# A circulant recurrence rebuilt: from a doubling tree over all sequences to one scan along time per sequence, pipelined over sequences

## The chip, the cores and the metric

The kernel runs on one NeuronCore of a Trainium2 chip. The metric is the device time of one launch in microseconds (us), taken as the median of several executions. Beside it there is one profiled execution, whose trace gives every instruction with its engine, its line in the kernel, its start and its duration. PE is TensorE (matmuls), DVE is VectorE, ACT is ScalarE, POOL is GpSimd and SP is SyncE, which issues DMAs here. All data is fp32.

## What is computed

Eight sequences of 512 tokens with 128 features (`u`) go through a chain of residual blocks: a linear recurrence with a circulant transition matrix, a LoRA feed-forward network, a four-layer encoder with linear attention, LoRA again, causal attention, a mixture of experts, a gated linear recurrence, and experts again. Only the first block changes:

```
z    = layernorm(x)
h_t  = W h_{t-1} + B z_t          # W orthogonal and circulant, 128 x 128
x   += C h_t + D z_t
```

`W` is the Cayley transform of a skew circulant matrix. Its eigenvalues are `(1 - w^2 - 2iw) / (1 + w^2)`, of modulus 1, with `w` from a Fourier sine sum over 63 parameters. In the Hartley basis (cosine plus sine) each frequency is a plain rotation by an angle, so powers of `W` are cosines and sines of multiples of that angle.

## The kernel before

`net_kernel` issues the input loads, runs `rotate_block` for the recurrence, then enters `encoder_block`, which holds LoRA and the encoder as pipelines over sequences. A pipeline (`pieces`) takes a generator for each sequence and a list of ages; in each round it advances several sequences by one step each, in the listed order, and after every so many steps it may advance a second stream, its `side`. LoRA runs with `LORA = (-2, 0, 1, -1, 0, -1, 1, -1, -2)`, and from its round 6 on the encoder's stream is its side. Inside `encoder_block` everything stands under `in_program_order`: each of PE, DVE, ACT and POOL executes its instructions in the order in which the code writes them.

`rotate_block` stands outside that order. It works on all eight sequences at once, in five parts:

- The norm of each sequence (`zin`, lines 169, 170, 156, 157, 187), the transpose to features by time (`flip`, L196, copied by L148) and the product with `B` (L234, copied by L150 into `h`).
- Cosine and sine of the rotation angle, starting from a matmul with the sine table (L242) and followed by small DVE operations (L243 to L249), then eight angle doublings (L253 to L258).
- Nine weight matrices, one for each power of two of `W` (L268 to L271 on DVE, L275 and L276 on PE, L277).
- A doubling tree along time: nine levels up and eight levels down, each a matmul (L287) and an addition (L288) on strided columns of `h`. The wide levels work on every second column, the narrow ones on one or a few columns per sequence.
- The output: products with `C` and with a diagonal of `D` (L301, L302), added to `x` (`add_x`, L219).

LoRA's steps on a sequence are the norm (`norm_start`, `norm_end`, where every second piece runs on ACT, L183), a bias added on POOL (L216), the transpose and four selections (L196, L333), `left` and `e` (L339, L341, L350), two small outer products (L356) added to the weights (`w1e` L359, `w2e` L360), then the network (L366, L367, L374) and `add_x`.

The queues at the start: SP issues `u` in eight parts (L2160), then the encoder's weights `e`, the blank fills of the expert slots (L966) and `l`. ACT's queue issues `ident`, `col`, `f` (LoRA's weights) and `a` (the recurrence's weights). POOL's queue issues `lnf`, `row` and `erow`. Rotation weights have a pool of their own (`w_a`). `ps` gives PSUM tiles; the usual banks are four of tag a, two of b and two of c.

Of the kernel before, what the change touches and what calls it, by code (L numbers as in the profile page):

```python
# [19 lines left out]
P = 128  # L20
B = 8
# [68 lines left out]
class Net:  # L90
# [30 lines left out]

    def load(self, name, pool=None, queue=None, parts=1, rows=None):

        dram = self.drams[name]
        n = dram.shape[1]
        if rows:
            dram = dram.to_broadcast([rows, n])
        t = (pool or self.const).tile([dram.shape[0], n], dram.dtype, name=f"w_{name}")
        step = -(-n // parts)
        for at in range(0, n, step):  # L130
            to = min(at + step, n)
            (queue or self.nc.sync).dma_start(t[:, at:to], dram[:, at:to])
        fields = {}
        for key, (at, shape) in self.offsets[name].items():
            v = t[:, at : at + math.prod(shape)]
            if len(shape) == 2:
                v = v.rearrange("p (a b) -> p a b", b=shape[1])
            elif len(shape) == 3:
                v = v.rearrange("p (a b c) -> p a b c", b=shape[1], c=shape[2])
            fields[key] = v  # L140
        self.packs[name] = fields
        return fields
# [16 lines left out]
    def norm(self, src, dst, n=NT, split=False):  # L159

        self.norm_end(src, dst, self.norm_start(src, n), split)

# [11 lines left out]
    def norm_end(self, src, dst, found, split=False):  # L174
# [6 lines left out]
        for t in range(n):  # L181
            if split and t % 2:
                nc.scalar.activation(  # L183
# [37 lines left out]

def rotate_block(k):

    nc, tc = k.nc, k.tc
    w = k.packs["a"]
    lv = 9
    with tc.tile_pool(name="rot", bufs=1, reuse_waits="tile") as pool, tc.tile_pool(name="rot_t", bufs=2, reuse_waits="tile") as tmp:
        h = pool.tile([P, B, S], F32, name="h")
        zt = pool.tile([P, B, S], F32, name="zt_all")
        for b in range(B):  # L230
            z = k.zin(b)
            k.flip(z, zt[:, b, :])
            pu = k.ps([P, S])
            nc.tensor.matmul(pu, w["bw"], zt[:, b, :], start=True, stop=True)  # L234
            k.evac(h[:, b, :], pu)


        cs = pool.tile([P, lv], F32, name="cs")
        sn = pool.tile([P, lv], F32, name="sn")
        t = pool.tile([P, 6], F32, name="eig")  # L240
        pp = k.ps([P, 1], "c")
        nc.tensor.matmul(pp, w["sin"], w["a"], start=True, stop=True)  # L242
        nc.vector.tensor_copy(t[:, 0:1], pp)  # L243
        nc.vector.tensor_tensor(t[:, 1:2], t[:, 0:1], t[:, 0:1], ALU.mult)
        nc.vector.tensor_scalar(t[:, 2:3], t[:, 1:2], 4.0, 1.0, ALU.mult, ALU.add)
        nc.vector.reciprocal(t[:, 3:4], t[:, 2:3])
        nc.vector.tensor_scalar(t[:, 4:5], t[:, 1:2], -4.0, 1.0, ALU.mult, ALU.add)
        nc.vector.tensor_tensor(cs[:, 0:1], t[:, 4:5], t[:, 3:4], ALU.mult)
        nc.vector.scalar_tensor_tensor(sn[:, 0:1], t[:, 0:1], 4.0, t[:, 3:4], ALU.mult, ALU.mult)  # L249
        sq = pool.tile([P, 2 * lv], F32, name="eig_sq")  # L250
        for i in range(1, lv):
            c0, s0 = cs[:, i - 1 : i], sn[:, i - 1 : i]
            nc.vector.tensor_tensor(sq[:, 2 * i : 2 * i + 1], s0, s0, ALU.mult)  # L253
            nc.vector.tensor_tensor(sq[:, 2 * i + 1 : 2 * i + 2], c0, c0, ALU.mult)
            nc.vector.tensor_tensor(
                cs[:, i : i + 1], sq[:, 2 * i + 1 : 2 * i + 2], sq[:, 2 * i : 2 * i + 1], ALU.subtract
            )
            nc.vector.scalar_tensor_tensor(sn[:, i : i + 1], c0, 2.0, s0, ALU.mult, ALU.mult)  # L258


        ra = pool.tile([P, lv, P], F32, name="ra")
        rb = pool.tile([P, lv, P], F32, name="rb")
        wt = pool.tile([P, lv, P], F32, name="wt")
        for i in range(lv):
            c0, s0 = cs[:, i : i + 1], sn[:, i : i + 1]
            u = tmp.tile([P, P], F32, name="u")
            v = tmp.tile([P, P], F32, name="v")
            nc.vector.tensor_scalar(u, w["sin"], s0, None, ALU.mult)  # L268
            nc.vector.scalar_tensor_tensor(ra[:, i, :], w["cos"], c0, u, ALU.mult, ALU.subtract)
            nc.vector.tensor_scalar(v, w["cos"], s0, None, ALU.mult)  # L270
            nc.vector.scalar_tensor_tensor(rb[:, i, :], w["sin"], c0, v, ALU.mult, ALU.add)  # L271
        for at in range(0, lv, 4):
            n = min(4, lv - at)
            pw = k.ps([P, n, P], "c")
            nc.tensor.matmul(pw, w["cos"], ra[:, at : at + n, :], start=True, stop=False)  # L275
            nc.tensor.matmul(pw, w["sin"], rb[:, at : at + n, :], start=False, stop=True)  # L276
            nc.vector.tensor_scalar(wt[:, at : at + n, :], pw, 1.0 / P, None, ALU.mult)  # L277

        def level(i, first, count):

            d = 1 << i
            seqs = min(max(1, S // count), B // 2)
            for b in range(0, B, seqs):
                to = h[:, b : b + seqs, first : first + (count - 1) * 2 * d + 1 : 2 * d]
                of = h[:, b : b + seqs, first - d : first - d + (count - 1) * 2 * d + 1 : 2 * d]
                ph = k.ps([P, seqs, count])
                nc.tensor.matmul(ph, wt[:, i, :], of, start=True, stop=True)  # L287
                nc.vector.tensor_tensor(to, to, ph, ALU.add)  # L288

        for i in range(lv):  # L290
            level(i, (2 << i) - 1, S >> (i + 1))
        for i in range(lv - 2, -1, -1):
            level(i, (3 << i) - 1, (S >> (i + 1)) - 1)

        dg = pool.tile([P, P], F32, name="dg")
        nc.vector.tensor_scalar(dg, k.ident, k.col["D"], None, ALU.mult)
        for b in range(B):
            py = k.ps([P, NT, D])
            for t in range(NT):
                at = slice(t * P, (t + 1) * P)  # L300
                nc.tensor.matmul(py[:, t, :], h[:, b, at], w["cw"], start=True, stop=False)  # L301
                nc.tensor.matmul(py[:, t, :], zt[:, b, at], dg, start=False, stop=True)  # L302
            k.add_x(b, py)

# [112 lines left out]
def encoder_block(k, before, behind):  # L417
# [7 lines left out]
    with tc.tile_pool(name="enc1", bufs=1, reuse_waits="tile") as one, tc.tile_pool(name="enc", bufs=2, reuse_waits="tile") as pool:  # L425
# [158 lines left out]
        with in_program_order(tc):  # L584
# [9 lines left out]
            stream = counted()  # L594
            before(pool, stream)
            for _ in stream:
# [1559 lines left out]
def net_kernel(ctx: ExitStack, tc: tile.TileContext, drams, offsets, out):  # L2156
    nc = tc.nc
    k = Net(ctx, tc, drams, offsets)
    for b in range(B):
        nc.sync.dma_start(k.xb(b), drams["u"][b].rearrange("(t p) d -> p t d", p=P))  # L2160
    k.ident = k.load("ident", queue=nc.scalar)["ident"]
    k.col = k.load("col", queue=nc.scalar)
    k.mhalf = k.const.tile([P, 8], F32, name="mhalf")
    nc.gpsimd.memset(k.mhalf, -0.5)
    k.lnf = k.const.tile([P, 2, D], F32, name="lnf")
    nc.gpsimd.dma_start(k.lnf.rearrange("p a d -> p (a d)"), drams["lnf"].to_broadcast([P, 2 * D]))
    k.all1 = k.const.tile([P, P], F32, name="all1")
# [8 lines left out]
    saved = tc.dram_tile([P, B * NT * D], F32, name="saved")  # L2176

    w_e, w_a = ExitStack(), ExitStack()
    p_e = w_e.enter_context(tc.tile_pool(name="w_e", bufs=1))
    p_a = w_a.enter_context(tc.tile_pool(name="w_a", bufs=1))  # L2180
    rooms, own, w_f = ExitStack(), ExitStack(), ExitStack()
    room = rooms.enter_context(tc.tile_pool(name="moe1", bufs=1, side="right", reuse_waits="tile"))
    p_l = own.enter_context(tc.tile_pool(name="w_l", bufs=1, side="right", reuse_waits="tile"))
    ready = p_l.tile([P, S], F32, name="zt0")
    k.load("f", w_f.enter_context(tc.tile_pool(name="w_f", bufs=1, side="right")), nc.scalar)
    work = ExitStack()
    work.enter_context(k.working())
    k.load("a", p_a, nc.scalar)
    k.row = k.load("row", queue=nc.gpsimd, rows=P)
    k.load("erow", p_e, nc.gpsimd, rows=P)  # L2190
    k.load("e", p_e, parts=2)
    usual = dict(a=4, b=2, c=2)
    banks = dict(attention=dict(a=1, b=1, c=1, s=2, o=1), after=dict(a=3, b=2, c=3), experts=dict(a=4, b=2, y=2), gated=usual)
    flat = k.x.rearrange("p t d -> p (t d)")

    with k.banks(**usual):
        rotate_block(k)
    w_a.close()
    slots = [blank_slots(k, one) for one in GROUPS]
# [11 lines left out]

    def before(pool, side):
        pipeline(lora_steps(k, lambda: pool), B, LORA, side=side, every=1, first=B - 2)

# [91 lines left out]
def _constants():  # L2306
# [4 lines left out]
    ang = 2.0 * np.pi * ((i[:, None] * i[None, :]) % P) / P  # L2311
    c["cos"], c["sin"] = np.cos(ang).astype(f), np.sin(ang).astype(f)
    pick = np.zeros((P, 4, 4), f)
# [40 lines left out]
def _layout(inp):  # L2354
# [10 lines left out]
    a = Pack(P)  # L2365
    a.add("cos", c["cos"])
    a.add("sin", c["sin"])
    a.add("bw", ae("B_w").T)
    a.add("cw", ae("C_w").T)
# [114 lines left out]
```

## Time and profile before

| | |
|---|---|
| median of 3 runs | 1958.11 us (1957.21 to 1969.49) |
| profiled execution | 1991.02 us, its span 1989.3 us, mean granted TensorE clock 0.921 |
| busy, share of the span | PE 86%, DVE 65%, ACT 48%, POOL 37% |
| last `add_x` of the recurrence (L219) | starts at 92.47 us |
| LoRA's first L366 | starts at 98.03 us |
| blank fills, issue on SP (L966) | 14.54 to 69.22 us |

The profile's views used here are the windows (busy time of each engine in stretches of the span, with the granted clock and the DMA rate), the timeline (instructions in order of time; the brackets give the idle time before an instruction and what ended it) and the groups (instructions of one line and shape: count, total busy us and mean ns after the bar, then the idle time before them). Durations and positions are those of the profiled execution, which took 1.7% longer than the median.

### The profile page before, as it was taken

What the parts mean: (1) busy time and instruction counts of PE and PEld (TensorE: products, weight loads), DVE (VectorE), ACT (ScalarE), POOL (GpSimd) and SP (SyncE); (2) the same over time, 40 slices, a digit from 0 to 9 for tenths busy, and PEclk for the clock granted to TensorE, in tenths of its full rate; (3) what the DMA queues carried; (4) which work ended last, traced back from release to release, by engine and by line L of the source; (5) the groups of instructions that cost most, each with busy time, mean ns of one, the idle gap of its engine ahead of it and who ended that gap; (6) DMA issues with size and microseconds to landing.
All of it is one profiled execution on the core that took longest, in us unless ns stands there. A gap on an engine that the chain in (4) does not pass through costs nothing.

```text
span 1989.3 us, 30025 instructions
## 1 busy us (share of the span) xinstructions
PE 1710.9 (86%) x10171; PEld 1164.1 (59%) x10171; DVE 1289.3 (65%) x4211; ACT 957.5 (48%) x1737; POOL 730.3 (37%) x866
## 2 busy tenths in 40 slices
PE   4998899999998798999989877888898878789895
PEld 2655678878776555444444445665555535567664
DVE  7666888888886765566667445337555784565463
ACT  1034556666654432566555543435544444454453
POOL 2022333333333522444444753643202216145543
PEclk9898999999998898899999889989998777899998
DMA  9800000000000011000000021122001001111341
GB/s 259 161 1 1 1 1 1 1 1 1 1 1 1 17 77 43 1 1 1 1 1 1 24 72 33 57 83 62 20 7 36 17 3 36 42 42 58 91 118 57
DMA packets 79391, 71.26 MB, mean 36 GB/s; under 512 B 6560, under 2 KB 73120, under 8 KB 78336
## 3 DMA queue, kind: packets, MB, share of 16 engines
q1 hardware_dynamic: 69120, 47.89, 9.7%
q0 software_dynamic: 9536, 20.47, 3.1%
q8 instruction: 86, 1.41, 0.3%
q10 hardware_dynamic: 576, 0.90, 0.1%
q14 instruction: 73, 0.60, 0.1%
HBM read 34.98 MB, written 34.25 MB: 35 GB/s over the span
## 4 chain that ended last, share of the span: by engine, by line
PE 29%; DVE 14%; ACT 7%; issue 5%; POOL 1%; another core or an unknown queue 1%; DMA 1%; DVEq 0%; POOLq 0%; ACTq 0%; SPq 0%
PE ps_a L1320 4%; PE ps_a L1321 3%; PE ps_s L715 3%; PE ps_y L1293 3%; PE ps_b L1284 2%; PE ps_o L744 2%; DVE sh L1709 2%; DVE x L1370 2%; PE ps_c L935 1%; ACT pr L725 1%; PE ps_a L1727 1%; DVE half L1333 1%; DVE hid L1334 1%; PE ps_a L1293 1%; PE ps_a L1878 1%
## 5 line engine op out<-in xcount | busy, mean ns | idle before, releaser
L157 POOL TENSOR_TENSOR ln_rs<-rs_v,mhalf 128x4 f32<-128x4 f32 x144 | 150.3, 1045 | 393.7 <-DVE rs_v L156 381.9
L1217 POOL DMA_INDIRECT given<-yr,to x163 | 158.8, 974 | 287.8 <-PE ps_a L1320 76.7
L1333 DVE SCALAR_TENSOR_TENSOR half<-half,ps_a 128x352 f32<-128x352 f32 x163 | 84.5, 518 | 202.7 <-ACT half L1326 163.4
L725 ACT ACTIVATE pr<-ps_s 128x1024 f32<-128x1024 f32 x160 | 154.7, 1019 | 125.7 <-PE ps_s L715 118.8
L1205 POOL DMA_INDIRECT slots<-xn,rpos x128 | 125.6, 981 | 84.3 <-issue 33.9
L1320 PE MATMUL ps_a<-w_m,xt 128*128 x326 | 135.7, 500 | 13.4 <-ACT xt L1266 12.4
L715 PE MATMUL ps_s<-qm,rot 32*128 32x128 f32 (+3 forms) x1024 | 124.3, 489 | 19.1 <-ACT pr L725 18.9
L1321 PE MATMUL ps_a<-w_m,xt 128*128 x326 | 133.1, 492 | 8.7 <-ACT yr L1296 7.8
L729 POOL TENSOR_SCALAR_AFFINE_SELECT pr<-pr 128x256 f32<-128x256 f32 x256 | 99.9, 416 | 106.2 <-ACT pr L725 102.1
L556 PEld LDWEIGHTS ps_c<-w_e,mlp_g 128*128 128x128 f32 x1024 | 126.7, 198 | 15.1 <-issue 14.8
L1286 ACT COPY gt<-ps_b 128x384 f32<-128x384 f32 x163 | 78.0, 479 | 116.0 <-PE ps_b L1284 86.1
L556 PE MATMUL ps_c<-w_e,mlp_g 128*128 128x128 f32 x1024 | 128.9, 281 | 0.1
L548 PE MATMUL ps_a<-zt,w_e 128*128 128x512 f32 x256 | 123.7, 607 | 0.9 <-ACT zt L203 0.9
L1326 ACT ACTIVATE half<-ps_a 128x352 f32<-128x352 f32 x163 | 75.8, 465 | 98.5 <-PE ps_a L1320 89.8
L1284 PEld LDWEIGHTS ps_b<-w_ident,hid 128*128 128x128 f32 x489 | 63.2, 147 | 91.6 <-DVE hid L1334 34.0
L1284 PE MATMUL ps_b<-w_ident,hid 128*128 128x128 f32 x489 | 85.5, 285 | 36.1 <-DVE hid L1334 26.5
L170 DVE BATCH_NORM_AGGREGATE ln_mv<-ln_st 128x2 f32<-128x6 f32 x576 | 102.6, 180 | 18.6
L715 PEld LDWEIGHTS ps_s<-qm,rot 32*128 32x128 f32 x1024 | 59.3, 193 | 78.0 <-ACT pr L725 52.5
L216 POOL TENSOR_TENSOR xe<-xe,w_erow 128x512 f32<-128x512 f32 x64 | 82.3, 1305 | 57.1 <-DVE ks L506 52.8
L549 ACT ACTIVATE mlp_g<-ps_a,w_col 128x512 f32<-128x512 f32 x128 | 85.7, 687 | 35.4 <-PE ps_a L548 35.4
L1334 DVE SCALAR_TENSOR_TENSOR hid<-half,ps_a 128x352 f32<-128x352 f32 x163 | 85.0, 521 | 22.1 <-PE ps_a L1321 3.5
L203 ACT ACTIVATE zt<-ps_b,w_col 128x512 f32<-128x512 f32 x80 | 62.7, 783 | 70.8 <-PE ps_b L196 70.8
(384 smaller groups left out, 3967.7 us busy)
## 6 DMA issues: line engine op xcount, KB each, us to landing
xr<-slots SPq DMA_DIRECT2D x37, 260.0 KB
y<-given SPq DMA_DIRECT2D x32, 256.0 KB
slots<-blank SPq DMA_DIRECT2D x3, 2535.0 KB
w_m<-in_m_dram SPq DMA_DIRECT2D x2, 2244.0 KB
w_e<-in_e_dram SPq DMA_DIRECT2D x2, 1700.0 KB
slots<-blank SPq DMA_DIRECT2D x2, 1495.0 KB
given<-yr,to POOLq DMA_INDIRECT x163
x<-in_u_dram SPq DMA_DIRECT2D x8, 256.0 KB
```

The source lines that it names most:

```text
L157: nc.gpsimd.tensor_tensor(out, v, self.mhalf[:, :n], ALU.pow)
L548: nc.tensor.matmul(ph, w1[:, c * P : (c + 1) * P], ht, start=True, stop=True)
L556: nc.tensor.matmul(py[:, t, :], g[:, c, t * P : (t + 1) * P], w2[:, c, :], start=(c == 0), stop=(c == 3))
L715: nc.tensor.matmul(halves[g // 2][:, g % 2, at : at + S - u * P], kr[rows, u * P : (u + 1) * P], qm[rows, i, u * P : S], start=True, stop= ...
L725: nc.scalar.activation(pr, sc, AF.Exp)
L1205: made = nc.gpsimd.indirect_dma_start(out=g.slots, out_offset=bass.IndirectOffsetOnAxis(ap=g.pos[:, i, t : t + 1], axis=0), in_=g.xn[:, t, :],
L1217: made = nc.gpsimd.indirect_dma_start(out=g.given, out_offset=bass.IndirectOffsetOnAxis(ap=to, axis=0), in_=yr, in_offset=None,)
L1284: nc.tensor.transpose(pt[:, q, :], hid[:, q, :], k.ident)
L1320: nc.tensor.matmul(pg, xt, w["experts"][:, bass.ds(o + HID, HID)], start=True, stop=True)
L1321: nc.tensor.matmul(pv, xt, w["experts"][:, bass.ds(o, HID)], start=True, stop=True)
L1333: nc.vector.scalar_tensor_tensor(half, half, 1.0, pg, ALU.add, ALU.mult)
L1334: nc.vector.scalar_tensor_tensor(flat, half, 0.5, pv, ALU.mult, ALU.mult)
```

## The change

`rotate_block` is replaced by `rotation_steps`, a pipeline of six steps over sequences with `ROTATION = (2, 0, -1, -3, 1, -2)`. It runs inside `encoder_block`, so in written order, and from its round 5 on it advances LoRA by one step after every three places: two LoRA steps a round, ten by its last round, 9. The recurrence is computed in the Hartley basis. Two matrices carry `z` into it (`into`), the result is multiplied with cosine and sine tables of every time step, one `tensor_tensor_scan` sums both products along time, POOL multiplies the sum with the same tables again, and two matrices (`outof`) carry it back through `C`. The tables `cs` and `sn` (128 frequencies by 512 steps) are built by nine doublings on DVE in `angles()`, the matrices in `weights()`.

The norm's second half goes to ACT entirely (`split=2`). Tables, products and matrices use tiles of the encoder's pool, and the pack `a` (with cosine-plus-sine tables in place of the cosine table, and `B` not transposed) is loaded into the unused tail of the encoder's `xe`. The loads of `f`, `row`, `erow` and `lnf` move to SP's queue, behind `u`; ACT's queue keeps `ident`, `col` and `a`.

```
-def rotate_block(k):
-    ...
+ROTATION = (2, 0, -1, -3, 1, -2)
+def rotation_steps(k, pool, free):
+    ...
+    def weights():
+        nc.tensor.matmul(pp, w["sin"], w["a"], start=True, stop=True)
+        pw = k.ps([P, 2 * P])
+        nc.tensor.matmul(pw, w["bw"], w["cas"].rearrange("p a b -> p (a b)"), start=True, stop=True)
+        nc.scalar.copy(into, pw)
+        pw = k.ps([P, 2, P])
+        for i in range(2):
+            nc.tensor.matmul(pw[:, i, :], w["cas"][:, i, :], w["cw"], start=True, stop=True)
+        nc.scalar.activation(outof, pw.rearrange("p a b -> p (a b)"), AF.Copy, scale=1.0 / P)
+    def angles():
+        ...
+        n = 1
+        while n < S:
+            m = min(n, S - 1 - n)
+            c, s = cs[:, n : n + 1], sn[:, n : n + 1]
+            of, to = slice(1, 1 + m), slice(1 + n, 1 + n + m)
+            u, v = ...
+            nc.vector.tensor_scalar(u, sn[:, of], s, None, ALU.mult)
+            nc.vector.tensor_scalar(v, cs[:, of], s, None, ALU.mult)
+            nc.vector.scalar_tensor_tensor(cs[:, to], cs[:, of], c, u, ALU.mult, ALU.subtract)
+            nc.vector.scalar_tensor_tensor(sn[:, to], sn[:, of], c, v, ALU.mult, ALU.add)
+            n *= 2
+    def steps(b):
+        x = k.xb(b)
+        found = k.norm_start(x)
+        if b == 0:
+            weights()
+        yield
+        z = k.work.tile([P, NT, D], F32, name="z")
+        k.norm_end(x, z, found, split=2)
+        yield
+        zt = ...
+        k.flip(z, zt, scale=1.0)
+        yield
+        ahead = []
+        for i in range(2):
+            pf = k.ps([P, S])
+            nc.tensor.matmul(pf, into[:, i * P : (i + 1) * P], zt, start=True, stop=True)
+            ahead.append(pf)
+        if b == 0:
+            angles()
+        back = ...
+        for by, pf, to in zip((cs, sn), ahead, back):
+            nc.vector.tensor_tensor(to, pf, by, ALU.mult)
+        total = pool.tile([P, S], F32, name="km")
+        nc.vector.tensor_tensor_scan(total, back[0], back[1], 0.0, ALU.add, ALU.add)
+        forth = ...
+        for by, to in zip((cs, sn), forth):
+            nc.gpsimd.tensor_tensor(to, total, by, ALU.mult)
+        yield
+        py = k.ps([P, NT, D], "c")
+        for t in range(NT):
+            at = slice(t * P, (t + 1) * P)
+            nc.tensor.matmul(py[:, t, :], zt[:, at], dg, start=True, stop=False)
+            for i in range(2):
+                nc.tensor.matmul(
+                    py[:, t, :], forth[i][:, at], outof[:, i * P : (i + 1) * P], start=False, stop=i == 1
+                )
+        yield
+        k.add_x(b, py)
+        yield
...
-    k.load("f", w_f.enter_context(tc.tile_pool(name="w_f", bufs=1, side="right")), nc.scalar)
+    k.load("f", w_f.enter_context(tc.tile_pool(name="w_f", bufs=1, side="right")))
-    k.load("a", p_a, nc.scalar)
-    k.row = k.load("row", queue=nc.gpsimd, rows=P)
-    k.load("erow", p_e, nc.gpsimd, rows=P)
+    k.row = k.load("row", rows=P)
+    k.load("erow", p_e, rows=P)
     k.load("e", p_e, parts=2)
+    nc.sync.dma_start(k.lnf.rearrange("p a d -> p (a d)"), drams["lnf"].to_broadcast([P, 2 * D]))
...
-    with k.banks(**usual):
-        rotate_block(k)
...
-    def before(pool, side):
-        pipeline(lora_steps(k, lambda: pool), B, LORA, side=side, every=1, first=B - 2)
+    def before(pool, free, side):
+        free = free.rearrange("p t d -> p (t d)")[:, (B - 2) * S :]
+        k.load("a", queue=nc.scalar, into=free)
+        after = pieces(lora_steps(k, lambda: pool), B, LORA, side=side, every=1, first=B - 2)
+        pipeline(rotation_steps(k, pool, free), B, ROTATION, side=after, every=3, first=5)
+        run(after)
```

## The prediction, made blind

> **What bounds the kernel now.** I read the share of each stage first, then the order of time inside the stage that changes, then single rows for prices. The windows of the profile (columns: stretch in us, length, busy us of each engine with instruction counts, granted TensorE clock, DMA share, GB/s) show where the recurrence is slow:
>
> ```profile
> 10.00:20.00 10.00, 0.59 (x2) 0.50 (x2) 6.62 (x48) 0.00 (x0) 3.05 (x3) 1.00 1.10 376
> ...
> 60.00:70.00 10.00, 10.00 (x41) 9.22 (x41) 4.17 (x20) 0.00 (x0) 0.00 (x0) 0.50 1.25 192
> 90.00:100.00 10.00, 8.35 (x41) 4.54 (x41) 6.38 (x17) 1.63 (x4) 0.11 (x1) 0.81 0.00 0
> 110.00:120.00 10.00, 9.13 (x55) 5.87 (x55) 6.69 (x22) 3.94 (x8) 2.25 (x3) 1.00 0.01 2
> ```
>
> In 10 to 20 us TensorE (first number after the length) does almost nothing: all eight norms are taken before the first matmul. In 60 to 70 it looks full, but with the narrow levels of the doubling tree, at half the clock. From 110 it is truly bound: LoRA repeats every 10.33 us with 9.13 us of TensorE. The timelines of VectorE (tree, then the end of the recurrence, then LoRA of sequence 0) and of TensorE give the edges:
>
> ```profile
> 61.69 0.19 DVE L288 TENSOR_TENSOR h<-h,ps_a 128x16 f32<-128x16 f32 x1 [0.19 <-PE ps_a L287]
> 62.19 0.18 DVE L288 TENSOR_TENSOR h<-h,ps_a 128x16 f32<-128x16 f32 x1 [0.32 <-PE ps_a L287]
> ...
> 92.47 0.69 DVE L219 TENSOR_TENSOR x<-x,ps_a 128x512 f32<-128x512 f32 x1 [1.10 <-PE ps_a L302]
> 93.45 0.70 DVE L339 TENSOR_SCALAR left<-ps_b,w_col 4x128 f32<-4x128 f32 x2 [0.29 <-PE ps_b L333]
> ...
> 98.14 0.69 DVE L360 TENSOR_TENSOR w2e<-w_f,ps_a 128x512 f32<-128x512 f32 x1 [1.34 <-PE ps_a L356]
> ```
>
> ```profile
> 94.98 3.12 PE L356 MATMUL ps_a<-e,left 4*128 4x512 f32 x4 [1.58 <-DVE e L341]
> 98.03 3.78 PE L366 MATMUL ps_a<-zt,w1e 128*128 128x512 f32 x4
> ...
> 111.87 1.98 PE L366 MATMUL ps_a<-zt,w1e 128*128 128x512 f32 x4
> 113.69 1.95 PE L374 MATMUL ps_c<-w2e,mlp_g 128*128 128x128 f32 x16
> ```
>
> So the recurrence owns 0 to 93 us: 20.5 before the first norm is applied, to 47.7 projecting and building the nine weights, the tree to 77.5, output to 92.5. LoRA of sequence 0 has its weights at 98.8, and runs cold until about 104 (L366 takes 3.78 for four matmuls; 1.98 warm). Everything after is written in order behind this. The chain of waits is followed back only to 845 us, so the order of time has to carry this.
>
> **Removed:** the tree's 76 matmul instructions and 32 additions, its weight building, the separate first pass over all norms.
>
> **Start of the new stage.** `a` is now third on ACT's queue instead of fourth, behind 100 KB instead of 620 KB. It landed at 13.2 (the wait at L242), about 876 KB through ACT's queue in roughly 11 us; the new `a` has 641 columns, 320 KB, and 420 KB at that rate land near 8 (bounds 6 and 13.2). Its load is the first thing ACT does, and TensorE's first matmul waits for it; behind that on TensorE are all transposes and behind the copies of `weights()` on ACT all norms. VectorE meanwhile takes norms 0 to 2. Under the written order one norm_start costs 1.8 us (4 x 0.395 between starts in the LoRA timeline, plus rs_v), so with x0 at 4.15 it is free for `angles()` at about 10.5. If `a` came at 13.2, at 14.
>
> **angles()**: five one-column steps took 0.9 (18.69 to 19.59), dg and memsets 0.3. Nine doublings of four instructions: the 128-wide quartet L268 to L271 took 0.92; narrow ones, each depending on the last, about 0.45; 255 wide about 1.6. Sum 5 x 0.45 + 0.5 + 0.65 + 1.0 + 1.6 = 6.0, all together 7.2: to 17.7. Nothing hides this on VectorE; TensorE waits behind it.
>
> **One round in the steady state** (one step each of six sequences):
> - TensorE: flip 0.53; two 512-wide matmuls as L366, 1.82 start to start; twelve 128-wide as L374, 8 for 1.78, so 2.68. Sum 5.03.
> - VectorE: add_x 0.70; two products from PSUM 0.61 + 0.72 (L359 and L360 start 0.61 apart); the scan 1.14 to 1.22; norm_start 1.80; nm 0.08. Sum 5.1.
> - ACT: four norm pieces 4 x 0.44 and the 0.59 copy, 2.4. POOL: two products at 1.27 and the power at 1.02, 3.6.
>
> ```profile
> L1800 DVE TENSOR_TENSOR_SCAN cum<-w_g,pol 128x512 f32<-128x512 f32 x4 | 4.9, 1224 | 0.1
> ...
> L216 POOL TENSOR_TENSOR x<-x,w_row 128x512 f32<-128x512 f32 x16 | 20.3, 1271 | 109.6 <-ACT z L183 109.6
> ```
>
> The scan row is another stage's, multiply then add; add-add is taken at the same price (bounds 0.7, an ordinary tensor_tensor, and 1.9, one and a half times the row; at 1.9 VectorE needs 5.8 a round, 4 us more in all). The longest loop across engines runs from nm, last on VectorE in a round, through ACT's 1.8, transposes 0.3 and `py` 2.7 to add_x, first on VectorE one round later: 5.0. Three limits near 5.1, so I take 5.3.
>
> **Two rules of the Trainium skill speak against this.** "GPSIMD Engine Reference", Engine selection: ordinary elementwise work with two inputs belongs on VectorE, as POOL is about half as fast. The rows agree on the price (1.27 against 0.69), but by the rule VectorE would have 6.3 a round, by the stage's rows POOL has 3.6 of 5.3 and nobody waits. The same page (Specifications) has POOL share its SBUF interface with VectorE instructions of two SBUF inputs, as the scan is. The row beside a busy VectorE: L216 mean 1.305, longest 1.715. Even at 1.7 each POOL stays at 4.4.
> "TensorE: Matmul & The Clock Gate", Part 1, The HAM clock gate: about 3.4 us idle halve the clock. Here 3.15 us idle before L275 at 41.99 went with a granted clock of 0.70 from 40 to 44. During `angles()` TensorE idles some 5 us, as flip 2 needs nm 2 behind them. By the rule `py` 0 runs at half rate, warm it would not: 3 us apart. I take half of that.
>
> **Sum.** Round 0: 17.7 + 4.4 (no add_x) = 22.1. Then flip 2 at 23.9, `py` 0 to 27.4 warm, 30.5 cold; taken 29. Rounds 2, 3, 4: 34.3, 39.6, 44.9. Round 5 has LoRA's norm of sequence 0 in place of the eighth, whose power waits behind POOL's products: 7.6, to 52.5. Round 6: 0.7 + 2.5 + 1.8, to 57.5. Round 7: 3.2, LoRA's left/e 2.7, wait for L356 0.9, w1e and w2e 1.3: 65.6. Before, the same w2e ended at 98.8: 33.2 earlier. The next mark, left/e of sequence 1, ends about 73.2 against 106.0: 32.8. From there LoRA is bound by TensorE as now, and the 33 us pass through.
>
> **Edits at nothing.** f, row, erow, lnf move to SP: four issues of about 0.55, so blank fills, `e` and `l` come about 2 us later. u's 2 MB stand ahead of them. First uses would be about 50 us for f and row (SP's issues are over near 17; f landed before 93 now, and with u ahead at 250 to 390 GB/s the estimate is 20), past 120 for erow, 784 for `l`. The cover gone would cost only what f is late, one for one. POOL loses three issues (1.9 us) that nothing waited for. The fills (near 200 GB/s to 80 us) lie beside the recurrence before and after. The borrowed tiles are freed before the encoder asks for them.
>
> **Against the measure.** The profiled execution took 1991.0 (span 1989.3), the median of the runs is 1958.1, ratio 0.983. 33 x 0.983 = 32.4: 1958.1 - 32.4 = 1925.7, say **1926**.
>
> **Rivals.**
> 1. *The rounds do not overlap well*: in order on four engines, each waits for another, 8 us instead of 5.3. For it: three limits within 0.1 us, and round 1 already waits for TensorE. Against: LoRA, built the same way, leaves TensorE idle only 0.87 of 10 us. Rounds 2 to 7: 6 x 2.7 = 16 less, 1942.
> 2. *Slower: TensorE at half clock through the whole stage.* Place: every round; price 5.0 each, 10.1 a round, over 8 rounds 40 - 33 = +7, 1965. It decides from 9.4 us a round. For it: 60 to 70 us above ran at 0.50. Against: that had matmuls of 4 to 64 columns; in 32 to 36 TensorE was busy 2.4 of 4 us with wide ones at 1.00, and at half clock it would be busy all the time, which opened the gate again at 104.
> 3. *The stage is hidden, or does not do what it says*: something later sets the time, 1958. Against: at 110 to 160 TensorE is bound while DMA moves 0 to 2 GB/s, so nothing but this order of work holds LoRA back.
>
> **Chances.** Forecast 0.80 (1916 to 1934: `a` at 6 to 13, rounds 5.1 to 5.7, py 0 warm or cold), rival 1 0.12, rival 2 0.04, rival 3 0.04. The range takes the forecast's bounds and part of rival 1: 1912 to 1943. A measurement tells about 1%, 19.6 us: faster takes the forecast and a third of rival 1, 0.84; same the rest of it and rival 3, 0.12; slower 0.04.
>
> **What would show it.** Right: first transposes near 12 us; scans about 5.3 apart at TensorE clock 1.00; w2e of sequence 0 at 62 to 70; LoRA again every 10.33. Wrong: `a` later than 13, products on POOL above 1.7, a scan of 1.9, or the first L356 of LoRA after 75 us.

## The result, and the profile after

| | before | after |
|---|---|---|
| median of 4 runs | 1963.8 us (1957.2 to 1970.0) | 1935.3 us (1934.7 to 1937.2) |
| ratio, 95% interval | | 0.9857 [0.9813, 0.9901] |
| profiled execution, its span | 1991.0, 1989.3 | 1934.7, 1932.9 |
| `w2e` of sequence 0 starts | 98.14 | 67.63 |
| `w2e` of sequence 1 starts | 107.28 | 78.73 |
| encoder's first matmul (L548, now L565) | 209.9 | 182.7 |
| attention's first matmul (L715, now L732) | 792.6 | 766.5 |
| first expert matmul (L1320, now L1337) | 1180.8 | 1157.1 |

The kernel became faster by 28.5 us between these medians. The forecast started from the median of three runs of the kernel before, 1958.1; with a fourth it is 1963.8, and against 1958.1 the gain is 22.8. In two later groups of runs the changed kernel stood 20.7 and 22.5 us below the kernel before. The forecast was 1926 with 1912 to 1943. It pointed the right way, and the gain is smaller than the 32.4 forecast.

The trace tells more than the totals, as the two profiled executions lie 56 us apart. LoRA of sequence 0 has its weights 30.5 us earlier, that of sequence 1 28.6, the encoder starts 27.2, attention 26.1 and the first expert stage 23.7 us earlier. The rest of the 56 us lies behind 1157 us, in the two expert stages, which the change doesn't touch: from the first expert matmul to the gated block's first one the profile before has 220.5 us, the profile after 202.4, and the second expert stage differs by about as much. Two experiments below tell whose effect this is: the kernel before with the new queues has 202.4 in the first expert stage, and the changed kernel with the old queues 202.5. So neither the recurrence nor the queues make the difference; it is scatter of these stages between executions or chips.

The same stretches of the windows as before (length, busy us of PE, PEld, DVE, ACT and POOL, granted clock, DMA share, GB/s), with 40 to 50 for a steady round:

```profile
10.00:20.00 10.00, 7.77 (x19) 3.69 (x18) 9.61 (x47) 4.90 (x12) 0.75 (x1) 1.00 0.94 371
...
40.00:50.00 10.00, 9.65 (x52) 6.06 (x52) 9.69 (x23) 4.26 (x10) 6.09 (x6) 1.00 1.30 174
...
60.00:70.00 10.00, 8.30 (x48) 6.05 (x47) 9.35 (x21) 0.90 (x3) 4.40 (x4) 0.95 1.27 186
...
110.00:120.00 10.00, 9.13 (x58) 6.20 (x56) 6.98 (x24) 3.44 (x6) 2.29 (x2) 1.00 0.00 1
```

From 10 to 20 TensorE now works (7.77 of 10 us, 0.59 before), and in 40 to 50 TensorE and VectorE are both busy for 9.65 us or more of 10, at full clock. LoRA in 110 to 120 is what it was. VectorE's timeline holds the steady round, from one `add_x` (L224) to the next, and GpSimd's timeline stands below it:

```profile
41.60 0.68 DVE L224 TENSOR_TENSOR x<-x,ps_c 128x512 f32<-128x512 f32 x1
42.20 0.68 DVE L301 TENSOR_TENSOR kp<-ps_a,qp 128x512 f32<-128x512 f32 x1
42.80 0.68 DVE L301 TENSOR_TENSOR kb<-ps_a,qp 128x512 f32<-128x512 f32 x1
43.51 1.23 DVE L303 TENSOR_TENSOR_SCAN km<-kp,kb 128x512 f32<-128x512 f32 x1
44.65 0.27 DVE L174 BATCH_NORM_STATS2 ln_st<-x 128x6 f32<-128x128 f32 x1
...
46.35 1.07 DVE L160 TENSOR_SCALAR rs_v<-ln_mv 128x4 f32<-128x4 f32 x1
47.33 0.15 DVE L185 SCALAR_TENSOR_TENSOR ln_nm<-ln_mv,ln_rs 128x4 f32<-128x4 f32 x1
47.41 0.68 DVE L224 TENSOR_TENSOR x<-x,ps_c 128x512 f32<-128x512 f32 x1
```

```profile
44.90 1.27 POOL L306 TENSOR_TENSOR qm<-km,qp 128x512 f32<-128x512 f32 x1 [2.14 <-DVE km L303]
46.13 1.27 POOL L306 TENSOR_TENSOR qr<-km,qp 128x512 f32<-128x512 f32 x1
```

A round takes 5.81 us. From start to start that is 0.60 + 0.60 + 0.71 + 1.14 + 1.70 (the statistics) + 0.98 (`rs_v`) + 0.08. VectorE has no gap, so no bracket shows a wait. But `rs_v` (the variance plus a small constant, ahead of the power on GpSimd) handles four numbers per partition, took 0.15 to 0.17 us in the recurrence before, and takes 1.07 here. It starts at 46.35, inside GpSimd's second product, and ends at 47.42; that product ends at 47.40. VectorE counts as busy while it is held. On TensorE the two ends of the stage read so:

```profile
8.20 0.59 PE L246 MATMUL ps_c<-xe 128*128 128x1 f32 x2 [8.20 <-DMA xe<-in_a_dram]
...
23.87 1.63 PE L201 MATMUL ps_b<-w_ident,z 128*128 128x128 f32 x4 [3.02 <-ACT z L188]
25.30 0.63 PE L311 MATMUL ps_c<-xe,hn 128*128 128x128 f32 x2
...
65.31 2.28 PE L373 MATMUL ps_a<-e,left 4*128 4x512 f32 x4 [1.66 <-DVE e L358]
...
71.13 0.63 PE L313 MATMUL ps_c<-at,qr 128*128 128x128 f32 x2
```

`a` lands at 8.2. After 3 us of idle, pairs of 128-wide matmuls take 0.63 instead of the 0.39 of the steady rounds (granted clock 0.50 from 25 to 27 us); the same comes back near 70 us (0.50 from 69 to 72).

### The profile page after: what moved, and what is told of

It reads as the page before. It is cut to its first block, busy times and chain, and to the rows that moved or that the text cites. A ratio compares the mean times of both kernels' runs of the same rounds, so it can differ in the third digit from the quotient of the medians.

```text
span 1932.9 us, 30021 instructions
## 1 busy us (share of the span) xinstructions
PE 1688.4 (87%) x10169; PEld 1157.8 (60%) x10169; DVE 1284.5 (66%) x4132; ACT 977.3 (51%) x1771; POOL 748.4 (39%) x879
## 3 DMA queue, kind: packets, MB, share of 16 engines
q1 hardware_dynamic: 69696, 49.67, 10.5%
## 5 line engine op out<-in xcount | busy, mean ns | idle before, releaser
L732 PE MATMUL ps_s<-qm,rot 32*128 32x128 f32 (+3 forms) x1024 | 124.8, 488 | 19.1 <-ACT pr L742 18.9
L1337 PE MATMUL ps_a<-w_m,xt 128*128 x326 | 132.1, 488 | 5.1 <-ACT xt L1283 4.7
L1338 PE MATMUL ps_a<-w_m,xt 128*128 x326 | 127.7, 474 | 8.4 <-ACT yr L1313 7.2
L565 PE MATMUL ps_a<-zt,w_e 128*128 128x512 f32 x256 | 123.7, 607 | 0.9 <-ACT zt L208 0.9
L175 DVE BATCH_NORM_AGGREGATE ln_mv<-ln_st 128x2 f32<-128x6 f32 x576 | 104.7, 182 | 19.7
L732 PEld LDWEIGHTS ps_s<-qm,rot 32*128 32x128 f32 x1024 | 58.9, 192 | 78.8 <-ACT pr L742 53.2
L221 POOL TENSOR_TENSOR xe<-xe,w_erow 128x512 f32<-128x512 f32 x64 | 82.3, 1305 | 56.7 <-DVE ks L523 52.5
L188 ACT ACTIVATE z<-x,ln_nm,ln_rs 128x128 f32<-128x128 f32 x96 | 41.2, 485 | 117.1 <-DVE ln_nm L185 117.1
L208 ACT ACTIVATE zt<-ps_b,w_col 128x512 f32<-128x512 f32 x80 | 62.7, 783 | 70.5 <-PE ps_b L201 70.4
```

What stands on the lines that cost most here:

```text
L175: nc.vector.bn_aggr(mv[:, t, :], st[:, t, :])
L565: nc.tensor.matmul(ph, w1[:, c * P : (c + 1) * P], ht, start=True, stop=True)
L732: nc.tensor.matmul(halves[g // 2][:, g % 2, at : at + S - u * P], kr[rows, u * P : (u + 1) * P], qm[rows, i, u * P : S], start=True, stop= ...
L1337: nc.tensor.matmul(pg, xt, w["experts"][:, bass.ds(o + HID, HID)], start=True, stop=True)
L1338: nc.tensor.matmul(pv, xt, w["experts"][:, bass.ds(o, HID)], start=True, stop=True)
```

## The experiments

**Theory.** The gain is the overlap: sequences follow each other in rounds that VectorE and TensorE nearly fill, the stage ends about 28 us earlier, and that is handed on. The gain falls short because `rs_v` on VectorE is held by GpSimd's products, and because TensorE runs at half clock at the stage's two ends. **Rivals:** the move of the loads brings the gain; the scan alone brings it, whatever the order; the rounds are bound by something else than `rs_v`.

Twelve runs, three groups, each beside the kernel before on the same chip. The third group ran on a slower chip; compare within groups, and small effects by marks in the trace.

**Yardsticks: the changed kernel again**

> The changed kernel again, as the yardstick of this group. The theory (the stage ends about 28 us earlier and hands that on one for one): 1930 to 1942 us, 24 to 32 us below the kernel before; rounds of 5.8 us; LoRA's weights of sequence 0 (w2e) end near 68.3. The rival (about half of the difference is the later stages' own variation): less than 20 us below it.

Measured: 1935.5 us beside 1956.1 before, ratio 0.9873 [0.9813, 0.9934], so 20.7 us: less than the 24 to 32 expected, and with this interval (13 to 37 us) not told from the rival's less than 20. The marks lie near those expected: `w2e` of sequence 0 starts at 68.80 (ends 69.5, 1.2 later), the encoder at 184.2.

> The changed kernel as the yardstick of this group: 1934 to 1937 us, w2e of sequence 0 ends 68 to 70, that of sequence 7 near 149.6.

Measured: 1973.95 beside 1996.5, ratio 0.9886 [0.9861, 0.9911], 22.5 us, again short of 24. The absolute time was missed: on this chip the kernel before is slower too (1996.5 against 1956.1 in the first group). Yet `w2e` of sequence 0 starts at 69.47 (ends 70.2, just out of the range) and that of sequence 7 at 149.8; the first expert matmul starts at 1159.3 in both yardsticks. The 38 us between them arise behind that.

**The queue moves alone, in the kernel before**

```
-    k.load("f", ..., nc.scalar)              # ahead of a
+    k.load("f", ...)
-    k.row = k.load("row", queue=nc.gpsimd, rows=P)
-    k.load("erow", p_e, nc.gpsimd, rows=P)
+    k.row = k.load("row", rows=P)
+    k.load("erow", p_e, rows=P)
     k.load("e", p_e, parts=2)
+    nc.sync.dma_start(k.lnf ...)             # was nc.gpsimd
```

> The kernel before with the queue moves alone: f, row, erow and lnf on SyncE's queue behind u, a third on ScalarE's; the doubling tree stays. Theory (the gain is the pipeline's; in the kernel before the norms of all sequences stand ahead of everything that needs a): 0 to 5 us below the kernel before, LoRA's first L366 at 93 to 98. Rival (the title's last words carry the gain, inputs first on their queue): 15 to 28 us below.

Measured: 1958.8 beside 1961.0, ratio 0.9987 [0.9963, 1.001]. TensorE's and VectorE's timelines of this run:

```profile
8.08 0.59 PE L242 MATMUL ps_c<-w_a 128*128 128x1 f32 x2 [8.08 <-DMA w_a<-in_a_dram]
11.18 2.27 PE L196 MATMUL ps_b<-w_ident,z 128*128 128x128 f32 x8 [2.51 <-DVE z L187]
```

```profile
96.91 0.69 DVE L360 TENSOR_TENSOR w2e<-w_f,ps_a 128x512 f32<-128x512 f32 x1 [1.32 <-PE ps_a L356]
```

`a` comes 5 us earlier and the first transposes 9.7 (they start at 20.91 in the profile before), and `w2e` only 1.2. What the tree needs next are its weights, and they start at 40.62 (L275), against 41.99: TensorE waits there for `ra`, which VectorE works out behind the norms of all sequences. The granted clock was lower on the way, too, 0.50 from 30 to 42 us (0.97 or more in the profile before), so part of the loss may be the clock's. The rival that the loads bring the gain falls.

**The old queues in the changed kernel**

```
-    k.load("f", ...)
+    k.load("f", ..., nc.scalar)              # ahead of a again
-    k.row = k.load("row", rows=P)
-    k.load("erow", p_e, rows=P)
+    k.row = k.load("row", queue=nc.gpsimd, rows=P)
+    k.load("erow", p_e, nc.gpsimd, rows=P)
-    nc.sync.dma_start(k.lnf ...)
+    nc.gpsimd.dma_start(k.lnf ...)           # first on its queue
```

> The pipeline as it is, with the loads in their old queues (f ahead of a on ScalarE's queue; lnf, row and erow on GpSimd's). Theory (a opens the stage, and the queue move is worth what a comes earlier): a lands at 12 to 13.5 instead of 8.2, the first transposes near 16, w2e of sequence 0 ends 72 to 73.5, the run 4 to 5 us above the changed kernel. Rival (the move of the loads carries most of the gain): 10 us or more above it. Rival (VectorE's norms and angles hide the load): 0 to 1 us.

Measured: 1938.65, against 1935.5 for the yardstick. TensorE's timeline starts here:

```profile
13.11 0.59 PE L246 MATMUL ps_c<-xe 128*128 128x1 f32 x2 [13.11 <-DMA xe<-in_a_dram]
```

`a` lands 4.9 us later than in the first profile after (13.11 against 8.20) and `w2e` of sequence 0 starts at 71.7, which is 4.1 later than there and 2.9 later than in the yardstick. At sequence 7 (151.4 against 148.9 in the yardstick) 2.5 us are left. The totals differ by 3.2, but their runs overlap (1935.1 to 1941.0 and 1931.4 to 1942.4), and at the first expert matmul the order is turned round (1156.8 against 1159.3). The theory's mechanism holds at LoRA, and its 4 to 5 us was too much. In the pipeline an early `a` is worth 2.5 to 3 us there; in the tree it was worth 1.

**All steps of a sequence in a row**

```
-ROTATION = (2, 0, -1, -3, 1, -2)
+ROTATION = (0, 0, 0, 0, 0, 0)
```

> The same instructions, but all six steps of a sequence stand one behind the other (all ages 0), so nothing of the recurrence overlaps with another sequence. Theory (the gain is the overlap; one sequence alone takes 1.8 norm + 1.0 power + 1.7 ScalarE + 1.0 transpose and copy + 2.5 into the basis and products + 1.2 scan + 2.5 GpSimd + 2.7 py + 0.6 = 15 us, up to 20 with TensorE at half clock): w2e of sequence 0 ends 145 to 175, the run 70 to 105 us above the changed kernel and 45 to 80 above the kernel before. Rival (the scan in place of the tree brings the gain, the order little): less than 20 us above the changed kernel, still below the kernel before.

Measured: 2023.4 us, ratio to the kernel before 1.0324 [1.0268, 1.038]; `w2e` of sequence 0 ends at 167.5. Eight scans lie between 17.7 and 155.6 us, 19.7 apart. VectorE's timeline, then the window of 50 to 60:

```profile
45.38 0.69 DVE L224 TENSOR_TENSOR x<-x,ps_c 128x512 f32<-128x512 f32 x1 [7.36 <-PE ps_c L313]
...
54.21 0.69 DVE L301 TENSOR_TENSOR kp<-ps_a,qp 128x512 f32<-128x512 f32 x1 [5.06 <-PE ps_a L295]
```

```profile
50.00:60.00 10.00, 6.20 (x12) 2.83 (x11) 2.61 (x3) 1.48 (x4) 1.97 (x2) 0.67 1.26 195
```

The same arithmetic, slower than the tree by 62 us: VectorE waits up to 7.4 and 5.1 us in each sequence, and TensorE, idle for 3.8 of these 10 us, gets 0.67 of its clock. The scan alone is no gain. The order is.

**No LoRA beside the last rounds**

```
-        pipeline(rotation_steps(k, pool, free), B, ROTATION, side=after, every=3, first=5)
+        pipeline(rotation_steps(k, pool, free), B, ROTATION)
```

> The recurrence's pipeline runs to its end before LoRA's first step is written; the rounds are as they are. Theory (the last five rounds hide LoRA's first ten steps; LoRA of sequence 0 then starts about 65 and needs some 9 us to its weights): w2e of sequence 0 ends 73 to 78, the run 5 to 10 us above the changed kernel. Rival (the LoRA steps in these rounds only lengthen them by what they take): 0 to 2 us above it.

Measured: 1945.6 us beside 1961.0, ratio 0.9935 [0.9906, 0.9964]. VectorE's timeline:

```profile
65.88 0.69 DVE L224 TENSOR_TENSOR x<-x,ps_c 128x512 f32<-128x512 f32 x1 [3.88 <-PE ps_c L313]
...
76.97 0.69 DVE L377 TENSOR_TENSOR w2e<-w_f,ps_a 128x512 f32<-128x512 f32 x1 [0.47 <-PE ps_a L373]
```

The recurrence is over at 66 instead of 72, but VectorE waits in its last rounds, and `w2e` comes 9.3 us later than in the profile after, at sequence 7 (154.6) 5.8. So some 6 us of the gain at sequence 7, and 8 to 9 at sequence 0, are the weaving of LoRA into the last rounds.

**The products behind the scan on VectorE**

```
-            nc.gpsimd.tensor_tensor(to, total, by, ALU.mult)
+            nc.vector.tensor_tensor(to, total, by, ALU.mult)
```

> The two products behind the scan run on VectorE instead of GpSimd. Theory (GpSimd's products cost VectorE 0.9 us a round by holding rs_v, two products on VectorE cost about 1.25): rs_v back at 0.17, rounds of 6.0 to 6.3 us instead of 5.8, w2e of sequence 0 ends 70 to 72, the run 1 to 4 us above the changed kernel. Rival (the rule that products of two inputs belong on VectorE; a shorter way to py pays): rounds below 5.8, the run 2 us or more below it.

Measured: 1939.0, beside 1961.0 before; the ratio, 0.9898 [0.9844, 0.9953], does not tell it from the changed kernel, so the round decides. VectorE's timeline:

```profile
37.16 0.68 DVE L224 TENSOR_TENSOR x<-x,ps_c 128x512 f32<-128x512 f32 x1
...
40.33 0.69 DVE L306 TENSOR_TENSOR qm<-km,qp 128x512 f32<-128x512 f32 x1
40.94 0.69 DVE L306 TENSOR_TENSOR qr<-km,qp 128x512 f32<-128x512 f32 x1
...
43.26 0.17 DVE L160 TENSOR_SCALAR rs_v<-ln_mv 128x4 f32<-128x4 f32 x1
...
43.41 0.68 DVE L224 TENSOR_TENSOR x<-x,ps_c 128x512 f32<-128x512 f32 x1
```

No product on GpSimd, and `rs_v` is back at 0.17. The round is 6.25 us: the two products cost more than the hold. `w2e` of sequence 0 starts at 73.1, later than expected. GpSimd is the better place for them, by 0.44 us a round.

**`rs_v` on ScalarE**

```
-        nc.vector.tensor_scalar(v, in_, scale, eps, ALU.mult, ALU.add)
+        nc.scalar.activation(v, in_, AF.Copy, scale=scale, bias=eps)    # in the recurrence only
```

> The recurrence's rs_v (variance plus epsilon) is computed on ScalarE instead of VectorE, all else as it is. Theory (only this VectorE instruction is held by GpSimd's products): VectorE loses it altogether, rounds of 4.9 to 5.2 us, w2e of sequence 0 ends 63 to 65, the run 3 to 5 us below the changed kernel. Rival (VectorE's next instruction is held in its place, whatever it is): rounds stay at 5.6 to 5.8.

Measured: 1935.6, no gain; `w2e` of sequence 0 starts at 70.4, against 68.8 in the yardstick. VectorE's and GpSimd's timelines:

```profile
37.85 0.67 DVE L227 TENSOR_TENSOR x<-x,ps_c 128x512 f32<-128x512 f32 x1
...
42.49 1.18 DVE L188 SCALAR_TENSOR_TENSOR ln_nm<-ln_mv,ln_rs 128x4 f32<-128x4 f32 x1
43.59 0.67 DVE L227 TENSOR_TENSOR x<-x,ps_c 128x512 f32<-128x512 f32 x1
```

```profile
42.38 1.26 POOL L309 TENSOR_TENSOR qr<-km,qp 128x512 f32<-128x512 f32 x1
```

The rival was right, and this run taught most. With `rs_v` gone from VectorE, the next instruction, `nm` (minus the mean times the inverse deviation), is held in its place: 1.18 us instead of 0.15, until GpSimd's product ends at 43.64. The round is 5.74. Not one instruction is at fault but whichever of this kind comes up while GpSimd multiplies. The statistics, which read one SBUF tensor, keep their 0.26 us beside GpSimd's products, and a product of VectorE that reads PSUM keeps its 0.69 (at 44.85 in the next run, inside GpSimd's of 44.47).

**The norm ahead of the scan**

```
-ROTATION = (2, 0, -1, -3, 1, -2)
+ROTATION = (2, -3, 0, -1, 1, -2)
```

> The norm's statistics stand ahead of the scan's step in each round, so that VectorE's rs_v no longer meets a product on GpSimd. Theory (rs_v is held by GpSimd's product for about 0.9 us a round): rs_v back at 0.17 us, rounds of 4.9 to 5.3 us instead of 5.8, w2e of sequence 0 ends 63 to 65 instead of 68.3, the run 3 to 5 us below the changed kernel. Rival (the rounds are bound by TensorE and by the loop through ScalarE, 5.0 to 5.8 us whatever VectorE does): rounds stay above 5.6 us and w2e above 67. A third way: the scan, now later in the round, delays py, and rounds grow beyond 6 us.

Measured: 1924.9 us (1924.5 to 1927.9), 10.6 below the yardstick; ratio to the kernel before 0.982 [0.9765, 0.9875]. VectorE's timeline, and GpSimd's second products of this round and of the next:

```profile
38.01 0.69 DVE L224 TENSOR_TENSOR x<-x,ps_c 128x512 f32<-128x512 f32 x1
...
40.34 0.23 DVE L160 TENSOR_SCALAR rs_v<-ln_mv 128x4 f32<-128x4 f32 x1
...
41.87 1.22 DVE L303 TENSOR_TENSOR_SCAN km<-kp,kb 128x512 f32<-128x512 f32 x1
43.01 0.14 DVE L185 SCALAR_TENSOR_TENSOR ln_nm<-ln_mv,ln_rs 128x4 f32<-128x4 f32 x1
43.20 0.69 DVE L224 TENSOR_TENSOR x<-x,ps_c 128x512 f32<-128x512 f32 x1
...
44.85 0.69 DVE L301 TENSOR_TENSOR kb<-ps_a,qp 128x512 f32<-128x512 f32 x1 [0.17 <-PE ps_a L295]
```

```profile
39.27 1.27 POOL L306 TENSOR_TENSOR qr<-km,qp 128x512 f32<-128x512 f32 x1
...
44.47 1.27 POOL L306 TENSOR_TENSOR qr<-km,qp 128x512 f32<-128x512 f32 x1
```

Now `add_x` and the statistics fill the time in which GpSimd multiplies, `rs_v` meets only the last 0.2 us of a product (0.23), and `nm` none. (In the first round and in the two that hold LoRA's norms, `rs_v` is still held, 0.90 to 1.07.) The round is 5.19 instead of 5.81, `w2e` starts at 64.16 instead of 68.80, at sequence 7 at 143.4 instead of 148.9: 5.5 us earlier. The run gained twice that, so it was run again:

> The norm ahead of the scan, once more. The local gain was 5.4 us at w2e of sequence 7, the run gained 10. Theory (the stages behind hand the gain on and the rest is their own scatter): 4 to 7 us below the changed kernel of this group. Rival (the later stages gain something of their own from the shift): again 9 to 12 us below.

Measured: 1967.6 against 1973.95, 6.3 us less; sequence 7 5.4 earlier (144.4 against 149.8). Ratios to the kernel before: 0.9853 [0.9823, 0.9883] and, for the yardstick, 0.9886 [0.9861, 0.9911]. So the reordering is worth some 5.5 us at LoRA, and 6.4 to 6.9 at the first matmuls of the encoder and of attention, in both groups. Whether the expert stages add a few of their own stays open.

**TensorE kept busy during the angles**

```
             ahead.append(pf)
+        if b == 1:
+            pd = k.ps([P, S], "c")
+            for i in range(3):
+                nc.tensor.matmul(pd, into[:, 0:P], zt, start=True, stop=True)
```

> The changed kernel with three extra 512-wide matmuls, whose result nobody reads, behind those of sequence 1 into the Hartley basis: they fill the 3.0 us in which TensorE idles during the angles. Theory (the idle halves the clock, py of sequence 0 then takes 4.1 us instead of 2.7, and add_x waits 1.16 us for it): TensorE keeps its full clock, py of sequence 0 ends 1.3 to 2 us earlier, the wait at the first add_x goes, w2e of sequence 0 ends 0.8 to 1.3 us earlier (66.5 to 68.5); in the whole run 0 to 2 us. Rival (VectorE is the bound here too and absorbs it): w2e at the same time within 0.3 us.

Measured: 1971.9 against 1974.0, not to be told apart in the total. TensorE's timeline and VectorE's first `add_x`, the yardstick of the group first:

```profile
23.91 1.64 PE L201 MATMUL ps_b<-w_ident,z 128*128 128x128 f32 x4 [3.80 <-ACT z L188]
25.34 0.64 PE L311 MATMUL ps_c<-xe,hn 128*128 128x128 f32 x2
```

```profile
30.63 0.69 DVE L224 TENSOR_TENSOR x<-x,ps_c 128x512 f32<-128x512 f32 x1 [2.23 <-PE ps_c L313]
```

```profile
20.38 2.74 PE L300 MATMUL ps_c<-zt,at 128*128 128x512 f32 x6
24.27 1.49 PE L201 MATMUL ps_b<-w_ident,z 128*128 128x128 f32 x4 [1.16 <-ACT z L188]
25.59 0.39 PE L315 MATMUL ps_c<-xe,hn 128*128 128x128 f32 x2
```

```profile
28.68 0.68 DVE L224 TENSOR_TENSOR x<-x,ps_c 128x512 f32<-128x512 f32 x1
```

With 1.2 us of idle instead of 3.8, `py` of sequence 0 runs at full rate throughout. The yardstick's first `add_x` waited 2.23 us for TensorE and starts at 30.63; here it starts at 28.68 without a wait. `w2e` starts at 67.6 against 69.5. The cold start costs up to 2 us there; against the first profile after, where the same `add_x` started at 29.52, it is 0.8, and `w2e` starts at 67.6 in both.

**The norm ahead, and LoRA woven in from round 3**

```
-ROTATION = (2, 0, -1, -3, 1, -2)
+ROTATION = (2, -3, 0, -1, 1, -2)
...
-        pipeline(rotation_steps(k, pool, free), B, ROTATION, side=after, every=3, first=5)
+        pipeline(rotation_steps(k, pool, free), B, ROTATION, side=after, every=3, first=3)
```

> The norm ahead of the scan, and LoRA's steps are woven in from round 3 on instead of 5, 14 of them by the end instead of 10. Theory (LoRA of sequence 0 has its weights only after the last rounds, TensorE waits 1.7 us for e there and then runs at half clock for some 5 us; earlier steps put this latency beside rounds that TensorE fills): rounds 3 and 4 longer by the LoRA work in them, the end of the recurrence up to 3 us later, but w2e of sequence 7 ends 2 to 5 us earlier than with the norm ahead alone (139 to 142), the run 2 to 5 us below it. Rival (TensorE and VectorE are full in these rounds, so the work only moves): within 1 us of it.

Measured: 1969.2, against 1967.6 with the norm ahead alone. `w2e` of sequence 0 starts at 61.0, four us earlier, but the last scan at 70.6 instead of 60.1, and `w2e` of sequence 7 at 149.4 instead of 144.4. The totals do not tell the two apart; the mark at sequence 7 does. The expectation was wrong: these rounds had no room. The work of LoRA lengthens them, and TensorE, after 4 us of idle, runs `py` at half rate near 55 us:

```profile
53.59 1.12 PE L201 MATMUL ps_b<-w_ident,z 128*128 128x128 f32 x4 [3.98 <-ACT zt L152]
54.50 0.63 PE L311 MATMUL ps_c<-xe,hn 128*128 128x128 f32 x2
```

Of the two, round 5 is the better place to start. The best version that ran is the norm ahead of the scan.

## Why the prediction was right, and which terms were mis-sized

The mechanism was as forecast. Its steps, predicted and measured in the profile after:

| step | predicted | measured |
|---|---|---|
| `a` lands | 8 | 8.2 |
| VectorE free for `angles()`, end of angles | 10.5, 17.7 | 9.64, 18.05 |
| round 0 ends | 22.1 | 23.2 |
| `py` of sequence 0 ends | 29 | 29.4 |
| rounds 2, 3, 4 end | 34.3, 39.6, 44.9 | 35.8, 41.6, 47.4 |
| round 5, round 6 end | 52.5, 57.5 | 55.0, 60.8 |
| `w2e` of sequence 0 ends | 65.6 | 68.3 |
| left/`e` of sequence 1 ends | 73.2 | 77.4 |

- **The term that failed is the contention.** The prediction named the SBUF interface that GpSimd shares with VectorE, and priced it on GpSimd: products slowed to 1.7 us, still hidden. In the runs the products keep their 1.26 to 1.27 us, and VectorE, the engine that sets the round, stands still for 0.9 us of it. In VectorE's sum for a round that is the step from 4.9 us, as the other rows came out (5.1 predicted; `add_x` took 0.6 instead of 0.7, the rest little less than forecast), to 5.81; the forecast had taken 5.3 for the whole round. "SBUF — State Buffer" of the Trainium skill, section "SBUF: two separate sides", has the rule that points to it: the shared port pair is an exclusive lock, and whoever starts first keeps it for the whole instruction. On VectorE's side the section names instructions with two SBUF inputs or in a performance mode of two ports. `nm` has two SBUF inputs; `rs_v` has one, and whether it ran in such a mode no run here shows. On the hold itself the runs agree: it ends with GpSimd's product to 0.1 us, it is gone when the products leave GpSimd (0.17), nearly gone when `rs_v` stands elsewhere in the round (0.23), and passes to `nm` when `rs_v` leaves VectorE. The trace of before had shown it too, in a group that the prediction did not read. These are VectorE's and GpSimd's timelines of the kernel before, in its encoder:

```profile
301.28 1.06 DVE L508 TENSOR_TENSOR kv<-kv,w_e 128x144 f32<-128x144 f32 x1
```

```profile
300.90 2.58 POOL L216 TENSOR_TENSOR xe<-xe,w_erow 128x512 f32<-128x512 f32 x2 [2.17 <-DVE ks L506]
```

  This product of two SBUF inputs takes 0.307 us at its shortest and 1.049 in the median there. All 25 of the 32 that take over 1 us start inside a product of GpSimd and end 0.15 to 0.17 us behind it; the six that take 0.31 meet none. A row whose median is three times its shortest deserved a question.
- **`angles()` took 8.4 us instead of 7.2.** The narrow doublings were priced 0.45 each and take 0.65: four instructions 0.13 to 0.15 apart, and a gap of 0.25 between one doubling and the next. Since VectorE was free 0.9 us earlier, only 0.35 remained of it.
- **The cold start** was taken at half of 3 us; it was that or more (29.4 measured; 1.2 to 2.2 us of wait at the first `add_x`). The rule that the prediction took there from "TensorE: Matmul & The Clock Gate", Part 1 (about 3.4 us idle halve the clock), is near what these runs show at this place: 3.0 and 3.8 us of idle ended in half rate, 1.2 did not. It did not foresee the half rate near 70 us, which came after 1.66 us of idle (last section).
- **The end was mis-sized by 1.5 us more.** The prediction let nearly all of the 33 us pass from sequence 0 to sequence 1 (65.6 to 73.2, 7.6 us). Measured are 9.1. Between the two, TensorE still owes the recurrence `py` of sequence 7 (67.5 to 71.5, mostly at half rate) before LoRA's first L383. From there on LoRA is bound by TensorE, and its `w2e` follow 10.0 to 10.3 us apart as before, but for one step of 12.0 beside another stretch at half clock (0.72 from 90 to 95 us), which the yardsticks do not have.
- **Passed on one for one:** right to within 2.5 us up to attention, 28.6 at sequence 1, 27.2 at the encoder and 26.1 there. At the first expert matmul 23.7 are left, near the 20.7 to 22.8 of the totals. From attention's first matmul to the experts' first the runs here take 387 to 392 us, whichever recurrence they have, so single executions do not say whether these last 2 us are lost or scatter. Scaling by 0.983 for the long profile was wrong in principle (most of the excess of that profile lay behind 1180 us, not in the stage), and worth only 0.6 us.
- **Small slips of the working:** the tree had 38 additions (L288), not 32, the terms of the loop across engines add to 4.8, not 5.0, and the blank fills were issued 2.6 us earlier (11.97), not later. None of them moves the sum.
- **The level** came out inside the range partly by luck: the kernel before lies anywhere from 1956 to 1964 in its medians on chips of this speed; on the slower chip of the third group both kernels stand 33 to 40 us higher. What the forecast can be held to is the gain, and that was 64 to 88% of the 32.4.
- **The edits at nothing** cost nothing: no first use waited for `f`, `row` or `erow`, and the queue moves give 1 us (tree) to 3 us (pipeline) at LoRA, through `a` alone.
- **The scan** took 1.22 us, as the gated block's row said. **Products on VectorE** would have given 6.3 a round by the prediction's sum, and gave 6.25: the decision to trust GpSimd's row was right, for a smaller margin than thought.
- **The rivals.** Rounds of 8 us did not come; they were 5.8. Half clock through the whole stage did not come either; the clock was full from 30 to 60 us. Much of it comes when the overlap is taken away (0.66 from 20 to 150 us), and then the kernel is slower than before, as that rival had it.

## What to carry to other kernels

When work goes to GpSimd beside a full VectorE, ask what VectorE executes in that very time, not only whether GpSimd has time for it. Instructions that read one SBUF tensor with statistics, or PSUM, ran on; a tiny instruction on SBUF alone stood until GpSimd's product was over. Reordering one place in the round was worth more here than the whole move of the loads, and an engine that is held counts as busy, so look for rows far longer than their size explains.

## What the runs showed of the hardware that was not expected

- VectorE's hold by GpSimd's products of 128x512: 0.15 to 0.17 us becomes 0.97 to 1.18, for a `tensor_scalar` with one SBUF input and for a `scalar_tensor_tensor` with several, whose data are four numbers per partition. GpSimd's own product was not longer by it.
- The profile shows no wait for this. The instruction is recorded as running.
- Half clock came back near 70 us without a long idle. TensorE was idle for 1.66 us, ran four matmuls with a contraction of only 4 rows (L373), and the granted clock fell to 0.50 at 68.9, in the middle of `py` of sequence 7. The four took 2.28 us, against 1.13 elsewhere, but not from the clock, which was 1.00 from 65 to 68: the second pair started at 66.47, when VectorE had written its half of `e` (L367, to 66.42), while elsewhere both pairs run side by side. Such matmuls alone did not bring the clock down: six later sets of four went by in the first yardstick at 1.00 from 74 to 140 us. What does, the idle time or both together, was not separated.
- Two chips reached the first expert matmul of the changed kernel at the same time, 1159.3 us, and the end 38 us apart: 200.8 against 218.9 us from the first expert matmul to the gated block, and more after it. Its cause stays open.
